# A chain of gated FFNs, attention and experts on one core: where cond's other-type half weights are loaded, which queue copies attention's values, when cond2's gate starts, and how the last tile ends

## The chip, the cores and the metric

The kernel runs on one core of a Trainium2 chip. A core has a matrix engine (TensorE, PE, with its weight loads shown as PEld), three elementwise engines (VectorE, DVE; ScalarE, ACT; GpSimd, POOL), and SyncE (SP), which here only issues DMA transfers. The letter q behind an engine's name marks its queue: instructions that wait, branch, count or issue transfers. All engines run side by side, each through its own instructions in order; a semaphore holds an instruction back until what it needs is done. The on-chip memory is addressed by 128 partitions, and the kernel lays it out by hand as one large tile (`arena`) that is cut into areas of 1 KB on each partition.

The metric is the device time of one execution in microseconds (us): the median over several runs. The profile comes from one more execution, whose own time is given beside it.

## What is computed

4096 tokens of 256 values, as 64 batches of 64. Every batch has a type from 0 to 2. All arithmetic is float32. The reference, cut to what matters here:

```python
def cond(x, t):                       # gated FFN, shared and by type
    share = (gelu(x @ sWi0) * (x @ sWi1)) @ sWo
    expert = (gelu(x @ Wi0[t]) * (x @ Wi1[t])) @ Wo[t]
    w = softmax(relu(concat([expert[:, 0], share[:, 0]]) @ g0) @ g1)
    return expert * w[:, 0] + share * w[:, 1]

def attn(x):                          # 16 heads of 16, causal, in each batch
    ...

def cond2(x, t):                      # three shared FFNs, two experts by type
    s0, s1, s2 = (relu(x @ share_wi[j]) @ share_wo[j] for j in range(3))
    out_a = relu(x @ wi[t]) @ wo[t];  out_b = relu(x @ wi[t + 1]) @ wo[t + 1]
    expert = out_a * wa + out_b * wb
    g = softmax(relu(concat([expert[:, 0], s0[:, 0], s1[:, 0], s2[:, 0]]) @ gate_w1) @ gate_w2)
    return expert * g0 + s0 * g1 + s1 * g2 + s2 * g3

def ffn(x):                           # router of three layers, top 2 of 8 experts
    scales = softmax(relu(relu(x @ rW1 + rb1) @ rW2 + rb2) @ rW3 + rb3)
    # each expert takes a limited number of tokens, adds its bias eb2, and is
    # weighted by its scale; the results are added at the token's row
    ...

x = x + attn(cond(x, itok))
x = x + ffn(cond2(x, itok))
```

## The kernel before

**Tiling.** The tokens are taken in `NSB` = 8 blocks of 512 (called s), sorted by type beforehand, so that a block has nearly one type. Each FFN layer is a product of blocks done by Strassen's method with seven products (the tiles `p1` to `p7`, with `sa`, `sb` for second halves; a letter behind them tells the stage: c for cond's shared FFN, e for cond's expert, d for cond2's, t for its expert, r for the router, m for the experts at the end). Sums of weight blocks are needed for that. They are made once on GpSimd by `sum_half` and written to DRAM (`sums_i`, `sums_o`, `sums_si`, ...; the store is L882, on GpSimd's own queue), and read back when a layer needs them. Sums of token blocks are made by `token_sums` (L193) on two engines, `eng` and `eng2`, with GpSimd taking `t3` and `t4` in most places.

**Stages, in PE's order.** cond's shared FFN (c); then `typed(0, 0)`, a few batches that are of another type than the rest of their block ("other types", plain matmuls without Strassen: tiles `peg`, `pel`, `e`); then cond's experts (e) for the eight blocks; cond2's first shared FFN (d0); the second (d1); other types of cond2 (`p2e`, `e`); the third (d2) and the experts (t); the router; the experts at the end (`pm`, `po`), whose rows are added into the output by a scatter.

**What sets the order.** The order is written out by hand. `pipeline(items)` (L402) runs the first half of item i + 1, then what is hung on item i by `hook`, then the second half of item i. Work that is not of the items, above all attention (queries, keys, values, scores, softmax, mixing) and the gates, is a list of small steps, `between`. `layer` (L300) calls `tick`, which takes one step off that list and puts it between two groups of matmuls. Empty steps `(None, False)` are spacers. The argument `ticks` ("fine", "late") says where in a layer those steps are put.

**The ring of half weights.** For cond, half weights come through a ring of `NRING1` = 5 slots of seven areas from `AT_RING1`. `queue1` (L941) lists them in order: 11 of the 12 pieces of the other types (`"f"`: k, q, and one of i0, i1, o), then the experts' pieces from the DRAM sums (`"m"`), the last `"f"` piece among them, then three of cond2's shared sums. `send1` (L948) loads the next one into the next slot: SP must wait until the piece that lay there has been used, and whatever is behind on SP's queue waits with it. In `typed(0, 0)`, `more()` calls `send1` whenever half a weight is done with.

**SP's queue.** Nearly all loads and stores go through `sync_dma` (L125) on SP's queue, one behind the other; `behind_last` keeps the written order.

**Attention's values.** For each pair of batches, `values(i)` (L1273) multiplies the values with two masks on GpSimd: `vx` (L1283) is copied across partitions into `vb` by two transfers of 64 KB on SP's queue (L1286), and the rest of `vb` is written by two multiplications (L1287). `mix` (the `ov` matmuls) reads `vb`; the softmax of the same pair runs meanwhile on VectorE (its last step is L1320). There are 32 such steps in the e and d0 stages.

**cond2's gate.** `combine2` (L1460) gives 21 steps for a block; its first, `hidden` (tile `phb`), reads first tokens that were loaded from `spillt`. For s from 1, six empty steps go ahead of it (L1622).

**The end.** `down` (L1921) finishes a tile of 128 rows of an expert: VectorE adds the bias (L1930), ACT scales by the token's weight (L1931), GpSimd issues the scatter that adds into the output (L1932). The last instruction of the kernel waits for that scatter (L1993).

Of the kernel before, what the change touches and what calls it, by code (L numbers as in the profile page):

```python
# [11 lines left out]
AF = mybir.ActivationFunctionType  # L12
# [47 lines left out]
AT_SHARE = (None, AT + 28, AT)  # L60
AT_HOPS2 = ((75, 95), (AT + 60, AT + 74), (AT_RING, AT_RING + 14))
AT_XSUM2 = (AT_XSUME, AT + 88, AT + 88)
AT_KEEP2 = ((62, 89), (AT + 92, AT + 96), (AT + 106, AT + 106))
AT_PARTS, AT_GW1, AT_X1 = AT + 92, AT + 104, 93
AT_GS = (170, AT + 112)

# [20 lines left out]
def adaln_attn_ffn(ctx: ExitStack, tc: tile.TileContext, a: dict, out: bass.AP):  # L87
# [105 lines left out]
    def token_sums(eng, eng2, b):  # L193
        b11, b12, b21, b22, t1, t2, t3, t4 = (b[n] for n in BLOCKS)
        eng.tensor_sub(t1, b12, b11)  # L195
        r = eng.tensor_sub(t2, b22, t1)  # L196
        eng2.tensor_sub(t3, b22, b12)  # L197
        return r.ins, eng2.tensor_sub(t4, b21, t2).ins  # L198

    def column_blocks(t, at, sums, eng=nc.gpsimd):  # L200
# [211 lines left out]
    def hook(it, *fs):  # L412
        it.between.extend(f for f in fs if f)
# [524 lines left out]
                q.append(("m", n - 1, "o"))  # L938
        return q

    queue1 = [("f", k, q, w) for k in range(NFIX) for q in range(2) for w in ("i0", "i1", "o")]  # L941
    last = queue1.pop()
    queue1 += in_order(0, 2 * NSB) + [("s", 1, "i"), ("s", 0, "o"), ("s", 1, "o")]
    queue1.insert(queue1.index(("m", 0, "i1")) + 1, last)
    ring1, types1, share0 = {}, {}, {}
    sent1 = [0]

    def send1():  # L948
        if sent1[0] == len(queue1):
# [26 lines left out]
    def typed(st, m):  # L976


        more = send if st else send1
        ac = []  # L980
        nn = 8 if st else 4
        hs = [0]
# [1 line left out]
        def item(b, n):  # L984
# [4 lines left out]
            def hidden(w, name):  # L989
                ph = bank(f"{name}{k}_{n}")  # L990
                for ff in range(2):
                    f = 2 * (q % 2) + ff
                    for c in range(DC):
                        mm(
                            ph[:, ff * BT : (ff + 1) * BT],
                            ring[st, k, j, q // 2, w][:, c, f * P : (f + 1) * P],
                            xes[st, k][0][:, c, :], c == 0, c == DC - 1,
                        )
                if q % 2:
                    more()  # L1000
                return ph

            def first():
# [12 lines left out]
            def second(h):  # L1016
                if not ac:
                    ac.extend(pair(f"e{st}_{m}_"))
                for ff in range(2):
                    f = 2 * (q % 2) + ff  # L1020
                    for c in range(DC):
                        mm(
                            ac[c][:, cols], ring[st, k, j, q // 2, "o"][:, f, c * P : (c + 1) * P],
                            h[:, ff * BT : (ff + 1) * BT], n == 0 and ff == 0, n == nn - 1 and ff == 1,
                        )
                if q % 2:
                    more()
                if b == 1 and n == nn - 1:
                    for c in range(DC):
                        nc.scalar.copy((tp if st else tp1)[:, c, :], ac[c])  # L1030
                    keep_typed(st, NB, NFIX * GB)
# [215 lines left out]
    def attention(s):  # L1247
# [25 lines left out]
        def values(i):  # L1273


            pv = bank(f"pv{s}_{i}")
            for c in range(DC):
                mm(pv[:, 0:D], cT[:, c, i * P : (i + 1) * P], aw["v"][:, c, :], c == 0, c == DC - 1)
            vn = area(AT_VN, D)
            nc.scalar.copy(vn, pv[:, 0:D])  # L1280
            vb = area(AT_VB + 2 * (i % 2), 2, D)
            vx = area(AT_VX + i % 2, D)
            nc.gpsimd.tensor_mul(vx, vn, K.vrest.rearrange("p a b d -> p (a b d)"))  # L1283
            for j in range(2):
                own, other = slice(64 * j, 64 * j + 64), slice(64 - 64 * j, 128 - 64 * j)
                nc.sync.dma_start(out=vb[other, j, :], in_=vx[own, :])  # L1286
                nc.gpsimd.tensor_mul(  # L1287
                    vb[own, j, :], vn[own, :], K.vmask[own].rearrange("p a b d -> p (a b d)")
                )
            return vb  # L1290
# [121 lines left out]
    def shared2(s, j):  # L1412
# [9 lines left out]
        def down(g):  # L1422
# [3 lines left out]

        return layer(
            f"d{s}_{j}", 2, ups, down, lambda: xblocks["d", s], AT_HOPS2[j], part,
            lambda: keep2(s, j, part), ahead, (AT_STE, AT_ST, AT_ST2)[j], ticks="late" if j or s > 3 else "fine",
        )  # L1430

    def store(g):
# [134 lines left out]
            between.extend(no + m2 + no * 2 + m3 + no + whole)  # L1567

    hook(items[13], lambda: [send1() for _ in range(NRING1 - 1)])
    more = []  # L1570
    for s in range(NSB):
        its = typed1(s, (lambda s=s: cut_e(s + 1)) if s + 1 < NSB else lambda: cut_x1(0, 0))
# [4 lines left out]
    starts = [10 + 2 * s for s in range(NSB)]  # L1577
    items += more
    n0 = len(items) - len(more)
    hook(more[0], send1)  # L1580
    hook(items[n0 + 2], begin_attention)
    for i in range(4):
        hook(more[3 + 5 * i], lambda v=halves2[3 - i]: sum_half(*v, AT_SUM2))
# [2 lines left out]
        share1 += shared2(s, 0)  # L1586
    items += share1
    for i in range(8):
        hook(share1[2 * i], lambda v=halves2[4 + i]: sum_half(*v, AT_RING1 + 7 * 3))
    for s in range(NSB):  # L1590
        hook(items[n0 + starts[s]], lambda s=s: begin_cond(s))
    hook(more[-2], lambda: send_share0("i", 0, AT_SUM2))
    for s in range(NSB):
        for i in range(2):
            hook(share1[2 * s + i], lambda g=NI * s + 2 * i: store(g))
# [19 lines left out]
    for s in range(NSB):  # L1615
# [3 lines left out]
            hook(its[1], lambda: [fetch2(0, j) for j in range(2)])  # L1619
            hook(its[2], router_weights, lambda: fetch2(0, 2))  # L1620
        else:
            hook(its[0], lambda s=s: between.extend([(None, False)] * 6 + combine2(s - 1)))  # L1622
        if s == NSB - 1:
            hook(its[2], lambda: sum_weights(nc.gpsimd, rw[0], 4))
            hook(its[4], router_weights1)
# [295 lines left out]
    def down(e, w, us=range(NU)):  # L1921
# [3 lines left out]
        for u in us:  # L1925
# [1 line left out]
            for f in range(FC):  # L1927
                mm(po, h[:, f, u * P : (u + 1) * P], wo[:, f, :], f == 0, f == FC - 1)
            eo = area(AT_EO + (e * NU + u) % 4, D)
            nc.vector.tensor_add(eo, po, b2[:, e, :])  # L1930
            nc.scalar.activation(eo, eo, AF.Copy, scale=xr[:, u, D + 1 : D + 2])  # L1931
            nc.gpsimd.indirect_dma_start(  # L1932
                out=out_rows, out_offset=bass.IndirectOffsetOnAxis(ap=row_i[:, u : u + 1], axis=0),
                in_=eo, in_offset=None, bounds_check=NB * S - 1, oob_is_err=False,
# [62 lines left out]
```

## Time and profile before

| | before |
|---|---|
| median of three runs | 2796.5 us (2794.85 to 2796.78) |
| the profiled execution's own time | 2799.37 us |
| its span | 2797.7 us |
| mean granted clock of TensorE | 0.997 |
| stretch 430 to 500 us: PE, DVE, POOL busy | 68.24, 51.76, 20.02 of 70 us |
| stretch 710 to 780 us: PE, DVE, POOL busy | 66.44, 58.63, 22.09 of 70 us |
| SP's longest waits in total at L1286 | 89.1 us for POOL L1283, 16 times |
| duration of the issues on SP at L1286 (64) | 502 / 572 / 4471 ns (least, median, most) |
| duration of the issues on GpSimd at L1410 (24) | 540 / 552 / 575 ns |

The profile gives, for every engine, its busy time as a share of the span; a list of the waits, each with what ended it; a timeline with the idle time ahead of each group of instructions; and the chain of waits, followed back from the last instruction. The granted clock is the share of full speed that the matrix engine was allowed in a stretch. A wait is attributed to one releaser even if several were late.

### The profile page before, as it was taken

The page shows a single profiled execution, that of the slowest core. Times are in us where ns is not written, and L with a number is a line of the kernel's source. Part 1 is how long each engine was busy: PE and PEld are TensorE (multiplying, and loading weights), DVE is VectorE, ACT ScalarE, POOL GpSimd, SP SyncE. Part 2 cuts the span into 40 slices and gives each one's busy share as a digit, 9 for nine tenths or more (in the row PEclk, how much of TensorE's full clock was granted, in tenths as well). Part 3 has the DMA queues.
Part 4 walks back from the last instruction along what each step waited for, and adds up shares of the span by engine and source line. Part 5 has one row for each costly group of instructions (what it writes and reads, how often), then busy time and mean ns, then how long its engine had stood idle before and what let it go on. Part 6 is the DMA issues. An engine that isn't in the chain of part 4 may idle for free.

```text
span 2797.7 us, 38593 instructions
## 1 busy us (share of the span) xinstructions
PE 2750.0 (98%) x13881; PEld 2269.0 (81%) x13881; DVE 1625.8 (58%) x2925; ACT 834.9 (30%) x1527; POOL 1031.3 (37%) x1057
## 2 busy tenths in 40 slices
PE   9999999999999999999999999999999999999998
PEld 7888877667676778888888888888888888887776
DVE  7777456878887774544546666667543333333443
ACT  2121114544443432211222222222222222221333
POOL 4655122322323656653332332236313232224332
PEclk9999999999999999999999999999999999999999
DMA  4454464333433223563244444444300000012330
GB/s 118 160 162 139 135 222 129 119 110 110 129 111 97 87 82 126 180 199 102 92 171 129 148 140 138 138 138 138 95 16 6 6 7 8 6 44 79 90 100 2
DMA packets 240463, 294.02 MB, mean 105 GB/s; under 512 B 142648, under 2 KB 204944, under 8 KB 240144
## 3 DMA queue, kind: packets, MB, share of 16 engines
q1 hardware_dynamic: 220752, 236.16, 27.2%
q0 software_dynamic: 19296, 54.35, 5.6%
q8 instruction: 110, 1.80, 0.3%
q10 hardware_dynamic: 224, 1.05, 0.1%
q14 instruction: 81, 0.66, 0.1%
HBM read 208.80 MB, written 84.25 MB: 105 GB/s over the span
## 4 chain that ended last, share of the span: by engine, by line
PE 85%; DVE 5%; DMA 4%; issue 3%; SPq 1%; ACT 1%; POOL 1%; POOLq 0%; DVEq 0%; ACTq 0%
PE sad L119 5%; PE p5r L119 5%; PE po L119 5%; PE p1r L119 5%; PE sbd L119 4%; PE sat L119 4%; PE p1d L119 3%; PE p5d L119 3%; PE sbt L119 3%; PE p7r L119 2%; PE p6r L119 2%; PE p4r L119 2%; PE p1e L119 2%; PE p5e L119 2%; PE p5t L119 2%
## 5 line engine op out<-in xcount | busy, mean ns | idle before, releaser
L197 POOL TENSOR_TENSOR arena<-arena 128x512 f32<-128x512 f32 (+1 forms) x175 | 236.5, 1352 | 853.1 <-DVE arena L195 666.0
L198 POOL TENSOR_TENSOR arena<-arena 128x512 f32<-128x512 f32 (+1 forms) x175 | 209.8, 1199 | 29.1 <-DVE arena L196 16.9
L119 PE MATMUL sad<-arena 128*128 128x256 f32 x768 | 177.1, 380 | 0.0
L119 PE MATMUL po<-arena 128*128 128x256 f32 (+1 forms) x704 | 169.8, 399 | 0.1
L119 PEld LDWEIGHTS sad<-arena 128*128 128x128 f32 x768 | 143.6, 190 | 19.6 <-issue 1.2
L119 PEld LDWEIGHTS po<-arena 128*128 128x128 f32 x704 | 132.7, 190 | 28.6 <-issue 11.2
L119 PE MATMUL p1r<-arena 128*128 128x256 f32 x640 | 150.2, 380 | 0.0
L119 PE MATMUL p5r<-arena 128*128 128x256 f32 x640 | 149.4, 380 | 0.5 <-DVE arena L255 0.5
L1813 POOL DMA_INDIRECT xs<-arena,slot_i x64 | 62.7, 979 | 200.5 <-ACT arena L1809 107.2
L119 PE MATMUL sbd<-arena 128*128 128x256 f32 x576 | 135.2, 382 | 0.0
L119 PEld LDWEIGHTS p5r<-arena 128*128 128x128 f32 x640 | 120.9, 190 | 17.2 <-DVE arena L255 1.1
L119 PEld LDWEIGHTS p1r<-arena 128*128 128x128 f32 x640 | 120.8, 190 | 17.3 <-issue 1.2
L195 DVE TENSOR_TENSOR arena<-arena 128x512 f32<-128x512 f32 (+2 forms) x127 | 95.1, 749 | 57.4 <-ACT arena L331 35.3
L188 POOL TENSOR_TENSOR arena<-arena 128x256 f32<-128x256 f32 (+1 forms) x53 | 49.5, 934 | 201.1 <-DMA arena<-in_L_cond_Wi 48.3
L119 PEld LDWEIGHTS sbd<-arena 128*128 128x128 f32 x576 | 108.0, 190 | 17.2 <-issue 3.0
L119 PE MATMUL sat<-arena 128*128 128x256 f32 x512 | 116.7, 381 | 0.6 <-POOL arena L197 0.6
L234 ACT COPY arena<-p1d 128x512 f32<-128x512 f32 x48 | 28.1, 586 | 295.3 <-PE p1d L119 291.5
L196 DVE TENSOR_TENSOR arena<-arena 128x512 f32<-128x512 f32 (+2 forms) x127 | 109.7, 864 | 3.2
L119 PEld LDWEIGHTS sat<-arena 128*128 128x128 f32 x512 | 96.6, 190 | 14.0 <-POOL arena L197 1.0
L1932 POOL DMA_INDIRECT out<-arena,rows_i x40 | 62.0, 1551 | 120.1 <-ACT arena L1931 64.3
L331 ACT ACTIVATE arena<-arena 128x512 f32<-128x512 f32 x144 | 90.1, 628 | 45.6 <-DVE arena L266 21.7
L119 PE MATMUL p5d<-arena 128*128 128x256 f32 x384 | 99.3, 381 | 3.3 <-DVE arena L255 3.3
(427 smaller groups left out, 6312.3 us busy)
## 6 DMA issues: line engine op xcount, KB each, us to landing
arena<-sums_i SPq DMA_DIRECT2D x32, 896.0 KB
arena<-sums_2i SPq DMA_DIRECT2D x32, 896.0 KB
arena<-sums_2o SPq DMA_DIRECT2D x32, 896.0 KB
arena<-in_L_ffn_eW SPq DMA_DIRECT2D x16, 1024.0 KB
arena<-sums_o SPq DMA_DIRECT2D x16, 896.0 KB
spill<-arena SPq DMA_DIRECT2D x24, 512.0 KB
arena<-spill POOLq DMA_DIRECT2D x24, 512.0 KB, 5.7
sums_i<-arena POOLq DMA_DIRECT2D x12, 896.0 KB, 4.0
```

What stands on the lines that cost most here:

```text
L119: nc.tensor.matmul(o, lhsT=lhsT, rhs=rhs, start=start, stop=stop, skip_group_check=shared_bank)
L188: eng.tensor_add(s1, a21, a22)
L195: eng.tensor_sub(t1, b12, b11)
L196: r = eng.tensor_sub(t2, b22, t1)
L197: eng2.tensor_sub(t3, b22, b12)
L198: return r.ins, eng2.tensor_sub(t4, b21, t2).ins
L234: nc.scalar.copy(s1, wide(x[1]))
L331: nc.scalar.activation(c_out(ij), src, AF.Relu)
L1813: nc.gpsimd.indirect_dma_start(out=to.rearrange("e n w -> (e n) w"), out_offset=bass.IndirectOffsetOnAxis(ap=slot_i[:, n, i : i + 1], axis=0),
L1932: nc.gpsimd.indirect_dma_start(out=out_rows, out_offset=bass.IndirectOffsetOnAxis(ap=row_i[:, u : u + 1], axis=0), in_=eo, in_offset=None, ...
```

## The change

It has seven parts.

1. `queue1` keeps five of the other types' twelve pieces (the first four, and the last). The other seven (`parts1`) are loaded by `send_parts`, hung on `items[14]`, into seven places of four areas from `AT` on, where cond's shared weights lay. `more(k, q, w)` in `typed(0, ...)` sends a next ring piece only if the half weight just finished lay in the ring; the single `send1` hung on `more[0]` goes. The ring has 56 pieces in place of 63, so pieces fall on other slots; two places that lie over ring slots move with them (`AT_KEEP2[0]` from 62 to 48, the area of `sum_half` from the fourth slot to the second).
2. The two copies of `vx` in `values` go out on GpSimd's queue in place of SP's. GpSimd's order in a step is then: multiply `vx`, multiply for `vb`, issue, issue, multiply for `vb`.
3. cond2's gate has seven empty steps ahead of it in place of six. With the gate's 21 steps that makes 28 for a block.
4. In `token_sums`, where one engine does all four (`eng is eng2`), `t3` comes behind `t2`: GpSimd does t1, t2, t3, t4 where it did t3, t1, t2, t4.
5. `send_share0("i", 0)`, a load of `sums_si` on SP's queue, is hung two items earlier.
6. The layer d0 puts its steps "late" from block 3 on; it did so from block 4 on. Attention's last steps fall elsewhere among the matmuls there.
7. The last tile of the last expert: ACT multiplies the bias by the token's weight ahead of time, into a spare area, and one VectorE instruction multiplies the matmul's result by the weight and adds that product, in place of an add on VectorE and a scaling on ACT.

```diff
--- before.py
+++ after.py
@@ -60,7 +60,7 @@
 AT_SHARE = (None, AT + 28, AT)
 AT_HOPS2 = ((75, 95), (AT + 60, AT + 74), (AT_RING, AT_RING + 14))
 AT_XSUM2 = (AT_XSUME, AT + 88, AT + 88)
-AT_KEEP2 = ((62, 89), (AT + 92, AT + 96), (AT + 106, AT + 106))
+AT_KEEP2 = ((48, 89), (AT + 92, AT + 96), (AT + 106, AT + 106))
 AT_PARTS, AT_GW1, AT_X1 = AT + 92, AT + 104, 93
 AT_GS = (170, AT + 112)
 
@@ -194,7 +194,8 @@
         b11, b12, b21, b22, t1, t2, t3, t4 = (b[n] for n in BLOCKS)
         eng.tensor_sub(t1, b12, b11)
         r = eng.tensor_sub(t2, b22, t1)
-        eng2.tensor_sub(t3, b22, b12)
+        with tc.issue_after(r.ins) if eng is eng2 else nullcontext():
+            eng2.tensor_sub(t3, b22, b12)
         return r.ins, eng2.tensor_sub(t4, b21, t2).ins
 
     def column_blocks(t, at, sums, eng=nc.gpsimd):
@@ -938,12 +939,18 @@
                 q.append(("m", n - 1, "o"))
         return q
 
-    queue1 = [("f", k, q, w) for k in range(NFIX) for q in range(2) for w in ("i0", "i1", "o")]
-    last = queue1.pop()
+
+    parts1 = [("f", k, q, w) for k in range(NFIX) for q in range(2) for w in ("i0", "i1", "o")]
+    queue1, parts1, last = parts1[:4], parts1[4:-1], parts1[-1]
+    in_ring = [*queue1, last]
     queue1 += in_order(0, 2 * NSB) + [("s", 1, "i"), ("s", 0, "o"), ("s", 1, "o")]
     queue1.insert(queue1.index(("m", 0, "i1")) + 1, last)
     ring1, types1, share0 = {}, {}, {}
     sent1 = [0]
+
+    def send_parts():
+        for i, (_, k, q, w) in enumerate(parts1):
+            send_half(0, k, 0, q, w, AT + 4 * i)
 
     def send1():
         if sent1[0] == len(queue1):
@@ -976,7 +983,12 @@
     def typed(st, m):
 
 
-        more = send if st else send1
+        def more(k, q, w):
+            if st:
+                send()
+            elif ("f", k, q // 2, w) in in_ring:
+                send1()
+
         ac = []
         nn = 8 if st else 4
         hs = [0]
@@ -997,7 +1009,7 @@
                             xes[st, k][0][:, c, :], c == 0, c == DC - 1,
                         )
                 if q % 2:
-                    more()
+                    more(k, q, w)
                 return ph
 
             def first():
@@ -1024,7 +1036,7 @@
                             h[:, ff * BT : (ff + 1) * BT], n == 0 and ff == 0, n == nn - 1 and ff == 1,
                         )
                 if q % 2:
-                    more()
+                    more(k, q, "o")
                 if b == 1 and n == nn - 1:
                     for c in range(DC):
                         nc.scalar.copy((tp if st else tp1)[:, c, :], ac[c])
@@ -1283,7 +1295,7 @@
             nc.gpsimd.tensor_mul(vx, vn, K.vrest.rearrange("p a b d -> p (a b d)"))
             for j in range(2):
                 own, other = slice(64 * j, 64 * j + 64), slice(64 - 64 * j, 128 - 64 * j)
-                nc.sync.dma_start(out=vb[other, j, :], in_=vx[own, :])
+                nc.gpsimd.dma_start(out=vb[other, j, :], in_=vx[own, :])
                 nc.gpsimd.tensor_mul(
                     vb[own, j, :], vn[own, :], K.vmask[own].rearrange("p a b d -> p (a b d)")
                 )
@@ -1426,7 +1438,7 @@
 
         return layer(
             f"d{s}_{j}", 2, ups, down, lambda: xblocks["d", s], AT_HOPS2[j], part,
-            lambda: keep2(s, j, part), ahead, (AT_STE, AT_ST, AT_ST2)[j], ticks="late" if j or s > 3 else "fine",
+            lambda: keep2(s, j, part), ahead, (AT_STE, AT_ST, AT_ST2)[j], ticks="late" if j or s > 2 else "fine",
         )
 
     def store(g):
@@ -1567,6 +1579,7 @@
             between.extend(no + m2 + no * 2 + m3 + no + whole)
 
     hook(items[13], lambda: [send1() for _ in range(NRING1 - 1)])
+    hook(items[14], send_parts)
     more = []
     for s in range(NSB):
         its = typed1(s, (lambda s=s: cut_e(s + 1)) if s + 1 < NSB else lambda: cut_x1(0, 0))
@@ -1577,7 +1590,6 @@
     starts = [10 + 2 * s for s in range(NSB)]
     items += more
     n0 = len(items) - len(more)
-    hook(more[0], send1)
     hook(items[n0 + 2], begin_attention)
     for i in range(4):
         hook(more[3 + 5 * i], lambda v=halves2[3 - i]: sum_half(*v, AT_SUM2))
@@ -1586,10 +1598,10 @@
         share1 += shared2(s, 0)
     items += share1
     for i in range(8):
-        hook(share1[2 * i], lambda v=halves2[4 + i]: sum_half(*v, AT_RING1 + 7 * 3))
+        hook(share1[2 * i], lambda v=halves2[4 + i]: sum_half(*v, AT_RING1 + 7))
     for s in range(NSB):
         hook(items[n0 + starts[s]], lambda s=s: begin_cond(s))
-    hook(more[-2], lambda: send_share0("i", 0, AT_SUM2))
+    hook(more[-4], lambda: send_share0("i", 0, AT_SUM2))
     for s in range(NSB):
         for i in range(2):
             hook(share1[2 * s + i], lambda g=NI * s + 2 * i: store(g))
@@ -1619,7 +1631,7 @@
             hook(its[1], lambda: [fetch2(0, j) for j in range(2)])
             hook(its[2], router_weights, lambda: fetch2(0, 2))
         else:
-            hook(its[0], lambda s=s: between.extend([(None, False)] * 6 + combine2(s - 1)))
+            hook(its[0], lambda s=s: between.extend([(None, False)] * 7 + combine2(s - 1)))
         if s == NSB - 1:
             hook(its[2], lambda: sum_weights(nc.gpsimd, rw[0], 4))
             hook(its[4], router_weights1)
@@ -1927,8 +1939,15 @@
             for f in range(FC):
                 mm(po, h[:, f, u * P : (u + 1) * P], wo[:, f, :], f == 0, f == FC - 1)
             eo = area(AT_EO + (e * NU + u) % 4, D)
-            nc.vector.tensor_add(eo, po, b2[:, e, :])
-            nc.scalar.activation(eo, eo, AF.Copy, scale=xr[:, u, D + 1 : D + 2])
+            by = xr[:, u, D + 1 : D + 2]
+            if e == E - 1 and u == NU - 1:
+
+                bw = area(AT_EO + (e * NU + u + 1) % 4, D)
+                nc.scalar.activation(bw, b2[:, e, :], AF.Copy, scale=by)
+                nc.vector.scalar_tensor_tensor(eo, po, by, bw, ALU.mult, ALU.add)
+            else:
+                nc.vector.tensor_add(eo, po, b2[:, e, :])
+                nc.scalar.activation(eo, eo, AF.Copy, scale=by)
             nc.gpsimd.indirect_dma_start(
                 out=out_rows, out_offset=bass.IndirectOffsetOnAxis(ap=row_i[:, u : u + 1], axis=0),
                 in_=eo, in_offset=None, bounds_check=NB * S - 1, oob_is_err=False,
```

## The prediction

> **What bounds the kernel now.** First the head of the page: the span, the share of each engine, and the chain that ended last.
>
> ```profile
> span 2797.7 us, 38593 instructions
> PE 2750.0 (98%) x13881; PEld 2269.0 (81%) x13881; DVE 1625.8 (58%) x2925; ACT 834.9 (30%) x1527; POOL 1031.3 (37%) x1057
> PE 85%; DVE 5%; DMA 4%; issue 3%; SPq 1%; ACT 1%; POOL 1%; POOLq 0%; DVEq 0%; ACTq 0%
> ```
>
> TensorE (PE) is the bound: 2797.7 - 2750.0 leaves 47.7 us without a matmul, start and end among them. The diff changes none of PE's work, so it can only gain from holes and from the half clock behind a long hole. So next the list of PE's waits, cut to those that the diff touches or could touch (what was waited for; us in total, times, longest):
>
> ```profile
> PE pel L119 <- DMA arena<-in_L_cond_Wi: 5.1, 1, 5.1
> ...
> PE ov L119 <- DMA arena<-arena: 2.9, 4, 1.1
> PE p6c L119 <- POOL arena L196: 2.5, 2, 2.0
> PE ov L119 <- ACT arena L1316: 2.0, 1, 2.0
> PE p1d L119 <- DMA arena<-sums_si: 1.9, 1, 1.9
> PE sae L119 <- POOL arena L197: 1.8, 1, 1.8
> PE phb L119 <- DMA arena<-spillt: 1.8, 2, 1.3
> ...
> PE phb L119 <- issue: 1.3, 1, 1.3
> ```
>
> One line or two for each edit; each is priced below from the timeline around it.
>
> **1. cond's other types out of the ring.** Seven half weights no longer wait for ring slots. The chain of waits before 356 is SP's queue: a block of eight 512 KB reads of `spill` (L126, 338.02 to 348.2), then the last half weight at 349.74, which takes 6.23 us to land. PE around it (start, us, instruction, count, idle before):
>
> ```profile
> 356.11 3.75 PE L119 MATMUL pel<-arena 128*128 128x256 f32 x8 [5.09 <-DMA arena<-in_L_cond_Wi]
> 359.65 2.70 PE L119 MATMUL e<-arena 128*128 128x256 f32 x6
> ...
> 363.92 1.89 PE L119 MATMUL pel<-arena 128*128 128x256 f32 x8
> ```
>
> The hole is 5.09 us. Behind it eight matmuls take 3.75 instead of 1.89 and six take 2.70 instead of 1.46 (the same six at 380.10): 1.86 + 1.24 = 3.1 us of low clock. Together -8.2. The new loads go to the areas of the shared weights, free after cond's last item, near 307 us; seven times 512 KB at the 272 GB/s seen in the window 350 to 364 is 13.5 us, so they have landed by about 328 us. Before, the pieces went out from 324.71 to 349.74 for use up to 356, so the cover is 20 us for the last and some microseconds for the first. What waits on SP behind them is a 0.38 us load (309.78) and stores at 323.44, both after the release. If the place came free late, the 8.2 would stay. What is late next: `pha` at 434.48 waits 1.48 for `spillt`, and stays.
>
> **2. The values' copies on GpSimd's queue.** SP loses 64 issues, GpSimd gets them, between its own multiplications (L1283, L1287). Now a copy stands behind whatever SP holds. First the SP queue, then PE, then the window with its granted clock ahead of DMA share and GB/s:
>
> ```profile
> 561.29 1.21 SPq L1286 DMA_DIRECT2D arena<-arena  x2
> ```
> ```profile
> 566.22 0.87 PE L119 MATMUL ov<-arena 128*32 128x64 f32 x16 [2.02 <-ACT arena L1316]
> ...
> 567.93 1.91 PE L119 MATMUL pv<-arena 128*128 128x256 f32 x4
> ```
> ```profile
> 566.20:570.60 4.40, 4.35 (x28) 3.23 (x30) 2.31 (x6) 1.49 (x3) 0.00 (x0) 0.61 0.98 343
> ```
>
> The wait is put down to ACT, but these copies, behind full DMA queues, landed at 566.1 and 566.4, just as `ov` starts: they end it. Waits for copies: 2.0 + 2.9 = 4.9 us. The clock of 0.61 over 4.40 us costs 4.40 x 0.39 = 1.7 (four `pv` take 1.91, four of the kind elsewhere 1.13). Together -6.6. In the later steps vx is ready 8 to 14 us before SP issues the copy (617.8 against 631.7); issued at vx, it has that much more time.
>
> The Trainium skill, "TensorE: Matmul & The Clock Gate", Part 1, has the clock halved only after an idle window of about 3.4 us. The row above disagrees, 0.61 after a hole of 2.02 us; by the rule this part would be worth 4.9 and the time 1.7 us longer.
>
> Against it stands GpSimd's time for an issue: 0.55 us by the nearest rows (L1410 552 ns, L882 573 ns), 64 x 0.55 = 35 us. In the attention stretches of 70 us GpSimd is busy 19 to 22 us, so its own 2 x 0.55 a step lie in idle time. The cost could come by VectorE, busy 57 of 70 us there:
>
> ```profile
> 719.06 5.33 DVE L1320 TENSOR_TENSOR arena<-arena,sm 128x512 f32<-128x512 f32 x2
> ```
> ```profile
> 719.38 0.58 POOL L882 DMA_DIRECT2D sums_si<-arena  x1 [0.30 <-POOL arena L191]
> ```
> ```profile
> 721.32 1.13 PE L119 MATMUL sae<-arena 128*128 128x256 f32 x4 [1.78 <-POOL arena L197]
> ```
>
> One of the two L1320 took 4.73 us (median 0.683) while GpSimd issued a store, and PE lost 1.78 and then 1.22 (`plga`, 724.53). Two other holes stand beside such issues: `p5d` at 931.58 (1.43) and 1014.95 (1.41). That is 5.8 us of PE in 38 issues of L882, and nothing in 24 of L1410. So 64 copies cost between 0 and 64 x 5.8 / 38 = 9.8. I take +3, nearer to L1410: these copies are small (64 KB) and have over 10 us in hand.
>
> **3. `send_share0` earlier, the gate later, t3 behind t2.** The load of `sums_si` goes out at 846.70 and ends PE's wait at 858.00; two items earlier is far more than 1.92 us: -1.9. The gate (`phb`, L1460 on) comes one tick later; a tick carries about four matmuls of 0.43 us, 1.7 us, more than the longest wait of 1.30: -3.1 for the three waits (1.30 at 1715.03, 1.28 at 1791.05, 0.48 at 1866.49). Its steps now fill all ticks of a stage, so a slip has nowhere to go; its fetches keep their place on SP. In `token_sums` on GpSimd the order:
>
> ```profile
> 80.70 1.17 POOL L197 TENSOR_TENSOR arena<-arena 128x256 f32<-128x256 f32 x1
> ```
> ```profile
> 84.08 1.13 PE L119 MATMUL p6c<-arena 128*128 128x256 f32 x4 [2.04 <-POOL arena L196]
> ```
>
> t3 (1.17) leaves the way to t1 and t2: -1.2 of that hole; the rest (the store's issue and t1, t2) stays.
>
> **4. Last tile in one step.** ACT's 0.51 leaves the way from the last matmul to the last scatter. But the chain at the end goes by the scatter before (start, us, what):
>
> ```profile
> 2786.86 2.72 DMA out<-arena,rows_i
> ...
> 2789.62 0.51 issue
> ```
>
> The last scatter (2790.36) follows that landing by 0.78, as the one before followed its own (2786.08 to 2786.86). Between -0.5 and +0.5 (a new ACT product, made before it is wanted); I take 0, since the spacing repeats.
>
> **5. What shifts.** Attention's remainder in the last pass is placed anew (`ticks="late"` from s = 3), one ring piece stands behind fetches, and the DVE holes (`p5c`, `p5d`, `sae`) come where chance puts them: 0, bounds -3 and +3 (that is the 721 event once more or once less).
>
> **Sum.** -8.2 - 6.6 + 3 - 1.9 - 3.1 - 1.2 = -18.0. The profiled execution took 2799.37 us, 1.67 around its span: 2799.4 - 18.0 = 2781.4. It lies 2.9 over the median of 2796.5; against that, **2778.5**. Own range: +6.8 (copies at 9.8), +-3, and 2.9 for the choice of execution: 2773 to 2788.
>
> **Rivals.**
> (a) GpSimd's issues starve VectorE in the 32 steps of the values. The 719 event is the price, 3.0 us; without the +3 the gains are 21.0, so from 7 steps on nothing is won, from 9 on (27) it is slower by over 0.2%, and at ten, -21 + 30, it is 2805. For: VectorE is 82% busy. Against: 24 issues of L1410 passed without it. The Trainium skill, "SBUF — State Buffer", section "Who interferes with whom", has an exclusive port of VectorE and GpSimd: an operation of VectorE with two SBUF inputs and one of GpSimd that reads SBUF block each other. The 4.73 us agrees, no row shows the lock itself. 0.09.
> (b) The waits for the copies pass to the next releaser (ACT's copies at L1316, DVE): the 6.6 is not had, 2785. For: that 2.02 is put down to ACT. Against: the landing times. 0.12.
> (c) Ring pieces that come later run dry. The i1 pieces of the later passes now follow eight `spillt` copies on SP, with 4.5 to 5 us left (issue 537.4, landing 542, use 547.0). Five of them late by 3 us each: 2793. For: SP's blocks of eight took 10 us at 338. Against: positive margin in every one. 0.07.
> (d) It doesn't do what it says: the parts' place is free too late, or its loads block SP, and the 8.2 stays: 2787. Against: 13.5 us of loading in 20. 0.05.
> (e) The holes at 721, 931 and 1015 go by the shift (-5.8) and the copies cost nothing (-3): 2770. 0.09.
>
> **How the numbers follow.** Forecast 0.58, rivals as given. 0.2% is 5.6 us, about what a measurement here can tell from none. Faster (under 2790.9): 0.58 + 0.12 + 0.05 + 0.09 = 0.84; same: (c), 0.07; slower: (a), 0.09. The range goes from (e) less 2 to (c): 2768 to 2793; (a) and some tails are left out.
>
> **What would show it.** No wait of `pel` near 350, and the clock full there; no `ov` wait over 0.3; `p1d` near 840 and `phb` without a hole; GpSimd's L1286 at about 0.55 us with L1320 near 0.68 beside it. The forecast is wrong if L1320 or other VectorE operations stretch beside L1286, if `e` or `p5e` wait for `sums_i`, or if `pel` still waits for `in_L_cond_Wi`.

## The result, and the profile after

The changed kernel takes 2779.15 us (median of six runs, 2776.67 to 2783.43), the kernel before 2796.64 in the same series (six runs, 2793.12 to 2799.43). The ratio is 0.9941, with a 95% interval from 0.9928 to 0.9954: between 13 and 20 us faster. The profiled execution took 2776.67 us, the fastest of the six. The profiled one of before, 2799.37, belongs to the earlier series and is as slow as the slowest of these six. So the two traces differ by more (22.7 us of span) than the medians (17.5).

The head of the page after:

```profile
span 2775.0 us, 38560 instructions
...
PE 2743.6 (99%) x13881; PEld 2265.6 (82%) x13881; DVE 1628.1 (59%) x2925; ACT 835.7 (30%) x1527; POOL 1065.5 (38%) x1121
```

PE still has 13881 matmul records, and 31.4 us of the span without one in place of 47.7. Its busy time fell too, by 6.4 us, with the same work: less of it ran at the low clock. Of PE's waits these are the ones that answer to the list of before:

```profile
PE pha L119 <- DMA arena<-spillt: 1.7, 1, 1.7
PE ov L119 <- ACT arena L1349: 1.6, 1, 1.6
PE p6r L119 <- DVE arena L196: 1.5, 6, 0.3
PE plga L119 <- DVE gha L1186: 1.4, 1, 1.4
PE sae L119 <- DMA arena<-sums_o: 1.3, 2, 1.0
```

`pel`, `p1d` and `phb` are gone; `ov` is not released by a copy any more in this list. Two kinds are new: six short ones of `p6r`, and two of `sae` for `sums_o`, a piece of the ring. Not shown are two kinds at the start, `px` (4.3, before 4.2) and one of 3.6, where PE came early to a step of the sort, and three of `ov` (1.8 in all) for which the profile names no releaser. The place of the 5.09 us hole, in PE's timeline (start, us, instruction, count):

```profile
351.23 1.89 PE L119 MATMUL peg<-arena 128*128 128x256 f32 x8
352.96 1.89 PE L119 MATMUL pel<-arena 128*128 128x256 f32 x8
354.68 1.89 PE L119 MATMUL e<-arena 128*128 128x256 f32 x8
```

Every group of eight takes 1.89 and follows the last without idle time. The last `pel` starts at 352.96, against 363.92 before; the first `peg` had started at 310.7, against 313.3. So this stage gave 8.3 us.

Where the 22.7 us between the two traces came from, by the starts of the same matmuls: 2.6 in cond's shared stage (not from the edits, see below), 8.3 in the other types, 7.4 from there to the first `p1d` (839.68 against 858.00), 1.6 up to cond2's gate, 3.1 at the gate (three `phb` holes), minus 1.6 from there to the last `po`, most of it in the router, and 1.4 behind the last matmul.

### The profile page after: what moved, and what is told of

It is laid out like the page before. It is cut to its first block, busy times and chain, and to the rows that moved or that the text cites. A ratio compares the mean times of both kernels' runs of the same rounds, so it can differ in the third digit from the quotient of the medians.

```text
span 2775.0 us, 38560 instructions
## 1 busy us (share of the span) xinstructions
PE 2743.6 (99%) x13881; PEld 2265.6 (82%) x13881; DVE 1628.1 (59%) x2925; ACT 835.7 (30%) x1527; POOL 1065.5 (38%) x1121
## 4 chain that ended last, share of the span: by engine, by line
PE 89%; DVE 4%; DMA 2%; issue 2%; SPq 1%; ACT 1%; POOL 1%; POOLq 0%; DVEq 0%; ACTq 0%
PE sad L119 6%; PE po L119 5%; PE p5r L119 5%; PE p1r L119 5%; PE sbd L119 4%; PE sat L119 4%; PE p5d L119 3%; PE sbt L119 3%; PE p1d L119 3%; PE p7r L119 2%; PE p6r L119 2%; PE p4r L119 2%; PE p5t L119 2%; PE p1t L119 2%; PE sac L119 2%; PE p5c L119 2%
## 5 line engine op out<-in xcount | busy, mean ns | idle before, releaser
L195 POOL TENSOR_TENSOR arena<-arena 128x256 f32<-128x256 f32 (+1 forms) x55 | 45.1, 820 | 245.5 <-ACT arena L1663 79.8
L119 PEld LDWEIGHTS p5r<-arena 128*128 128x128 f32 x640 | 120.8, 190 | 17.5 <-DVE arena L256 1.5
L188 POOL TENSOR_TENSOR arena<-arena 128x256 f32<-128x256 f32 (+1 forms) x53 | 48.9, 924 | 182.3 <-DMA arena<-in_L_cond_Wi 45.3
L332 ACT ACTIVATE arena<-arena 128x512 f32<-128x512 f32 x144 | 90.3, 628 | 42.3 <-DVE arena L267 22.7
```

What stands on the lines that cost most here:

```text
L119: nc.tensor.matmul(o, lhsT=lhsT, rhs=rhs, start=start, stop=stop, skip_group_check=shared_bank)
L188: eng.tensor_add(s1, a21, a22)
L332: nc.scalar.activation(c_out(ij), src, AF.Relu)
```

## The experiments

Twelve kernels ran, each in five rounds beside the kernel before. The table gives medians and ratios to that kernel in the same series. The changed kernel stood at 0.9941 in its own series; it was not timed again in the later ones.

| kernel | us | before | ratio, 95% interval |
|---|---|---|---|
| parts_alone | 2795.03 | 2795.99 | 0.9997, 0.9987 to 1.0007 |
| copies_alone | 2796.98 | 2795.99 | 1.0000, 0.9989 to 1.0010 |
| small_three | 2794.87 | 2795.99 | 0.9998, 0.9988 to 1.0008 |
| tile_and_late | 2798.19 | 2795.99 | 1.0012, 1.0002 to 1.0022 |
| both_parts_copies | 2786.14 | 2796.64 | 0.9962, 0.9949 to 0.9975 |
| copies_pinned | 2789.20 | 2796.64 | 0.9971, 0.9958 to 0.9984 |
| copies_twice | 2808.03 | 2796.64 | 1.0036, 1.0022 to 1.0050 |
| copies_on_sp | 2795.30 | 2796.64 | 0.9999, 0.9986 to 1.0011 |
| issues_more | 2796.47 | 2794.53 | 1.0008, 0.9998 to 1.0017 |
| late_back | 2783.83 | 2794.53 | 0.9958, 0.9944 to 0.9971 |
| fetch_later | 2785.76 | 2794.53 | 0.9967, 0.9955 to 0.9979 |
| t3_back | 2781.76 | 2795.21 | 0.9950, 0.9936 to 0.9964 |

**Each part alone.** The first four put one part, or a few, into the kernel before.

parts_alone has the first part of the diff and nothing else; its core:

```diff
+    queue1, parts1, last = parts1[:4], parts1[4:-1], parts1[-1]
...
+    hook(items[14], send_parts)
...
-    hook(more[0], send1)
```

> The kernel before with part 1 alone (the seven half weights in a place of their own, and the two places that move with the ring's slots). My theory: no wait of pel near 350, full clock there, about -8.2 us against the kernel before, so a ratio near 0.997. Rival: the hole only moves to the next load that SP holds up (pha near 434, or sae waiting for sums_o), and less than 4 us is left.

copies_alone:

```diff
-                nc.sync.dma_start(out=vb[other, j, :], in_=vx[own, :])
+                nc.gpsimd.dma_start(out=vb[other, j, :], in_=vx[own, :])
```

> The kernel before with part 2 alone (the values' copies on GpSimd's queue). My theory: -6.6 of waits and clock, +3 of GpSimd against VectorE, -3.6 in all (ratio 0.9987). Rival one: GpSimd's issues cost nothing, -6.6 (0.9976). Rival two: GpSimd's issues stretch VectorE's operations, 0 or slower, with L1320 over 2 us in several steps. Rival three: the waits of ov pass to ACT's copies, about 0 to -2 with ov waits of the same sum.

small_three:

```diff
-        eng2.tensor_sub(t3, b22, b12)
+        with tc.issue_after(r.ins) if eng is eng2 else nullcontext():
+            eng2.tensor_sub(t3, b22, b12)
...
-    hook(more[-2], lambda: send_share0("i", 0, AT_SUM2))
+    hook(more[-4], lambda: send_share0("i", 0, AT_SUM2))
...
-            hook(its[0], lambda s=s: between.extend([(None, False)] * 6 + combine2(s - 1)))
+            hook(its[0], lambda s=s: between.extend([(None, False)] * 7 + combine2(s - 1)))
```

> The kernel before with the gate a step later, send_share0 two items earlier and t3 behind t2. The forecast's terms: -3.1 -1.9 -1.2 = -6.2 (ratio 0.9978). From the profile after a rival: t3's order also removes three p5c holes in cond's stage (0.72, 1.72, 0.94), so -9.5 (0.9966), with no p5c wait on VectorE near 109, 154 and 194. If those holes are chance, they or others like them are there in this trace.

tile_and_late:

```diff
-(AT_STE, AT_ST, AT_ST2)[j], ticks="late" if j or s > 3 else "fine",
+(AT_STE, AT_ST, AT_ST2)[j], ticks="late" if j or s > 2 else "fine",
...
+                nc.scalar.activation(bw, b2[:, e, :], AF.Copy, scale=by)
+                nc.vector.scalar_tensor_tensor(eo, po, by, bw, ALU.mult, ALU.add)
```

> The kernel before with the last tile in one step and the layer d0 late from block 3. Forecast: 0 within 3 us (ratio 0.999 to 1.001); the last scatter still follows the landing of the one before by about 0.78 us. Rival: the placing of attention's last steps closes or opens holes of p5d near 930 and 1015, up to 3 us either way; and if ACT's 0.51 was on the way, the stretch from the last matmul to the end is shorter by it.

None of them was measurably faster, and the last was slower by 0.6 to 6 us. Added up they come to about +1 (-1.0, +1.0, -1.1, +2.2), where all together give -17.5. For the two large parts the traces show where gain is lost again. In parts_alone the hole at 350 is gone, as forecast, but a later one opens. PE's timeline of parts_alone:

```profile
487.48 1.13 PE L119 MATMUL sae<-arena 128*128 128x256 f32 x4 [2.81 <-DMA arena<-sums_o]
```

and SP's queue before it:

```profile
464.31 10.12 SPq L126 DMA_DIRECT2D arena<-spillt  x8
475.62 0.38 SPq L126 DMA_DIRECT2D arena<-sums_i  x1
476.11 1.23 SPq L1297 DMA_DIRECT2D arena<-arena  x2
477.58 0.39 SPq L126 DMA_DIRECT2D arena<-sums_i  x1
478.21 0.35 SPq L126 DMA_DIRECT2D arena<-sums_o  x1
```

The same stretch of SP's queue in the kernel before:

```profile
475.25 10.50 SPq L126 DMA_DIRECT2D arena<-spillt  x8
486.00 0.50 SPq L126 DMA_DIRECT2D arena<-sums_i  x1
486.60 1.22 SPq L1286 DMA_DIRECT2D arena<-arena  x2
488.05 0.39 SPq L126 DMA_DIRECT2D arena<-sums_o  x1
```

In parts_alone the piece that `sae` needs stands behind eight loads of `spillt`, two copies and two other pieces; it lands at 487.4. The ring's order moved by one piece, so three pieces now come behind that block where two did. With the clock behind the hole, 4.3 us of the 8.2 are given back there. The copies' wait at 561 is longer (2.77 in place of 2.02), but the clock stays full behind it, so nothing more is lost there. This does not yet give the median of -1.0: the trace is of the fastest execution of parts_alone (2790.27) and ends 9.1 us ahead of the trace of before. What takes the rest in the other executions, no trace shows.

copies_alone loses at the same place for another reason. PE's timeline of copies_alone, and the window with its granted clock ahead of DMA share and GB/s:

```profile
483.56 2.75 PE L119 MATMUL sbe<-arena 128*128 128x256 f32 x12
492.00 2.05 PE L119 MATMUL sae<-arena 128*128 128x256 f32 x4 [5.69 <-DMA arena<-sums_o]
```
```profile
492.00:497.70 5.70, 5.70 (x28) 3.89 (x28) 0.00 (x0) 0.59 (x1) 0.00 (x0) 0.50 0.00 0
```

5.69 us of hole and then half the clock: against the kernel before, 10.1 us are lost within 20 us. The weights are not late here (they land at 491.9, before at 494.4); the matmul is early. In the kernel before it stands behind `p4e`:

```profile
493.01 1.13 PE L119 MATMUL p4e<-arena 128*128 128x256 f32 x4
493.98 0.60 PE L1332 MATMUL ppT<-ident,arena 128*128 128x128 f32 x4
494.42 1.13 PE L119 MATMUL sae<-arena 128*128 128x256 f32 x4
```

The order of the engines' instructions is settled when the kernel is built, and in copies_alone this one product was put 76 matmuls further forward; PE's order is otherwise the same. Behind 500 the gains are there: 3.9 us at the hole of 566, then 0.8 near 637 and near 779, 2.3 up to the first `p1d` and 1.0 near 908, where the `ov` and `p1d` holes had been, with 1.1 lost near 725 and about 2 near 1015.

**Do the two parts need each other, and is it that one product?** both_parts_copies joins the edits of the first two. copies_pinned is copies_alone with the product held where it was:

```diff
                 for p in ("p1", "p6"):
-                    product(p)
+                    with tc.issue_after(pinned["p4e2_11"]) if (name, g) == ("e2", 1) else nullcontext():
+                        product(p)
```

copies_on_sp is the changed kernel with the copies back on SP's queue. copies_twice is a try at the price of GpSimd's issues:

```diff
-                nc.gpsimd.dma_start(out=vb[other, j, :], in_=vx[own, :])
+                for _ in range(2):
+                    nc.gpsimd.dma_start(out=vb[other, j, :], in_=vx[own, :])
```

> The kernel before with parts 1 and 2 together, nothing else. Singly they measured -1.0 and +1.0 us. Theory one (they need each other: alone, each meets a late ring piece near 490 that gives its gain back, 4.3 and 10.1 us there; together sae waits under 1.5 us there): -8.2 - 9.6 + 1 to 4, about -15, ratio 0.9935 to 0.996. Theory two (single effects add): 0 within 3 us.

> The kernel before with part 2 alone, and one product of sae (block 2, second item) held behind the p4 of its item, so that the matrix engine's order is that of the kernel before. Theory one (part 2 alone loses its gain only because that product was moved some 30 matmuls forward, ahead of its weights): the 5.69 us wait near 492 goes, and the kernel is 7 to 10 us under the one before (ratio 0.9965 to 0.9975). Theory two (the copies on GpSimd's queue cost by themselves): 0 within 3 us, with the wait at another instruction.

> The changed kernel with the copies back on SP's queue, all else as changed. Additive theory (part 2 alone was worth nothing): as the changed kernel within 3 us, 2779. Theory of the shared queue: sae near 487 waits 2.5 to 3 us again and loses some clock (4.3), ov waits near 561 and in four later places come back (6 to 9), so 2789 to 2792.

> The changed kernel with each of the 64 copies issued twice on GpSimd's queue (the second writes the same bytes again). It doubles GpSimd's issues and the small transfers. The forecast's price of GpSimd's issues against VectorE was +3 (bounds 0 and 9.8), so +3 us against the changed kernel, 2782 in all; if the issues are free, +0 to +1; if they starve VectorE, up to +10, with L1332 or other operations of VectorE over 2 us beside L1298.

Theory one holds for copies_pinned, and in direction for both_parts_copies. Together the parts give -10.5 (interval -7 to -14) where their sum singly is 0; the expected -15 was too much, and its trace has a `sae` wait of 3.1 near 562 besides the 1.0 near 483. With the product held, the copies alone give -7.4 (-4 to -12), PE's order is that of the kernel before, and this matmul starts without a wait:

```profile
490.64 0.60 PE L1334 MATMUL ppT<-ident,arena 128*128 128x128 f32 x4
491.08 1.03 PE L119 MATMUL sae<-arena 128*128 128x256 f32 x4
```

Taking the copies out of the changed kernel costs 16 us (2795.3), not 0, and more than the 10 to 13 expected: `sae` waits 2.7 near 490 and `ov` 2.8 near 564, as in parts_alone. So on SP's queue the copies and the ring's pieces hold each other up. The first part lets PE run earlier, and alone it meets a late piece; the second gets the pieces out earlier. The second does not need the first: alone it lost only by the product that moved. What the first adds to it is the difference of -10.5 and -7.4, about 3 us with intervals that overlap. No run takes part 1 alone out of the changed kernel.

copies_twice was far slower than any theory had it, 29 us over the changed kernel. GpSimd's timeline of copies_twice, and PE's waits:

```profile
560.78 0.54 POOL L1299 DMA_DIRECT2D arena<-arena  x1 [4.48 <-DMA arena<-arena]
```
```profile
PE ov L119 <- DMA arena<-arena: 11.4, 4, 3.5
```

The second transfer writes the same bytes, so GpSimd held it until the first had landed, 4.48 us here, and the other copy of the step stood behind it. That is a wait in a queue. So this run does not price the issues.

**The price of the issues, what is left near 485, and parts 6 and 4.** issues_more gives the changed kernel 64 more transfers without that wait:

```diff
                 nc.gpsimd.dma_start(out=vb[other, j, :], in_=vx[own, :])
+                nc.gpsimd.dma_start(out=aside[2 * (i % 4) + j], in_=vx[own, :])
```

late_back puts `s > 3` back:

```diff
-ticks="late" if j or s > 2 else "fine",
+ticks="late" if j or s > 3 else "fine",
```

fetch_later moves the loads of `spillt` of blocks 1 to 7 behind the three ring pieces, with the product near 490 held as above:

```diff
-            fetch_typed(0, s)
+            if s == 0:
+                fetch_typed(0, s)
...
     def begin_cond(s):
+        if s:
+            fetch_typed(0, s)
```

t3_back:

```diff
-        with tc.issue_after(r.ins) if eng is eng2 else nullcontext():
-            eng2.tensor_sub(t3, b22, b12)
+        eng2.tensor_sub(t3, b22, b12)
```

> The changed kernel with 64 more transfers of 64 KB issued on GpSimd's queue, each beside one of the copies, into a place in device memory that nobody reads (extra work, without the wait of one copy for the other that the doubled copies had). The forecast's price of the issues: +3 us (bounds 0 and 9.8) against the changed kernel's 2779, so 2782. If issues cost nothing on the path: 2779 to 2780, and VectorE's busy sum grows by less than 5 us. If they starve VectorE: over 2785, with VectorE's operations stretched beside L1298.

> The changed kernel with the layer d0 late from block 4 again (part 6 undone). From the run of the last tile with part 6 (+3.4 us against the kernel before): if that was part 6, this is about 3 us faster than the changed kernel, 2776, with p5d waiting near 1000 and no ov wait over 1.2 near 1008. If part 6 only trades one hole for another, 2779 within 2.5.

> The changed kernel with fetch_typed of blocks 1 to 7 put behind the three ring loads that it holds up on SP's queue (hung on begin_cond), and the product of sae near 490 held where it is in the changed kernel. If late ring pieces behind that block are what is left near 485 and 546: the sae wait of 0.96 and the ov wait of 1.01 go, with some clock, so 2 to 4 us faster, about 2776. If the fetch is then late for pha (20 us in hand before, some 10 then), a wait of pha appears in blocks 1 to 7 and it is slower.

> The changed kernel with t3 ahead of t1 and t2 on GpSimd again (part 2 of the order alone undone, the edit in token_sums). The forecast's term: 1.2 slower than the changed kernel, 2780. From the traces: the hole of 2.04 at 84 that the term came from is missing in six traces, five of them without the edit, and the edit brings six holes of p6r in the router (1.5 in all), which are in no trace without it; so 1 to 2 us faster, 2777 to 2778, and no p6r wait on VectorE past 2000. Either is under what five rounds tell apart; the holes in the trace decide.

issues_more came to 17 us over the changed kernel by medians of two series, and by neither theory. VectorE was not starved: its busy sum is 1632.6, 4.5 us more. PE's waits in that trace, then ACT and GpSimd around the longest:

```profile
PE p4d L119 <- ACT arena L1293: 4.7, 1, 4.7
...
PE plga L119 <- DVE gha L1187: 3.5, 1, 3.5
PE sc L119 <- ACT arena L1293: 3.3, 6, 1.0
```
```profile
925.39 0.37 ACT L1293 COPY arena<-pv 128x256 f32<-128x256 f32 x1 [5.66 <-POOL arena L1301]
```
```profile
922.39 0.59 POOL L1299 DMA_DIRECT2D arena<-arena  x1
922.97 0.57 POOL L1300 DMA_DIRECT2D aside<-arena  x1
923.54 0.52 POOL L1299 DMA_DIRECT2D arena<-arena  x1
924.05 0.53 POOL L1300 DMA_DIRECT2D aside<-arena  x1
924.64 0.72 POOL L1301 TENSOR_TENSOR arena<-arena,vmask 64x256 f32<-64x256 f32 x1
```

The second multiplication of a step stands behind all its issues, in this case four times 0.55 us. ACT's copy of the next values waits for it (`vn` must be read first), `p4d` waits for ACT, and so do six `sc`. Two issues a step, as in the changed kernel, still fit: there is no wait of PE for ACT L1292, the same copy, in its trace. In fetch_later two issues did not fit in one place: `p5d` waits 2.98 at 896 for the same copy (L1295 there), where GpSimd had also waited 1.14 for a transfer. The other 3.5, at `plga`, is not from the copies: a VectorE operation of 0.68 us stretched there to 4.83, as at 719 before. Of the 19.6 us between the spans of this trace and that of the changed kernel, some 7 lie at `p4d` and the low clock behind it, 4.5 at `plga`, 2.4 behind the last matmul (see the last section), and the rest in short waits.

late_back is 4.7 us over the changed kernel by medians of two series (10.7 against 17.5 under before), but the two intervals overlap, so part 6 stays unsettled; tile_and_late, with part 6 and the last tile in the kernel before, went the other way. In the traces part 6 trades a `p5d` hole near 1006 (1.41) for an `ov` hole near 1008 (1.61).

fetch_later was half right: both `sae` waits are gone, and no `pha` wait appears in blocks 1 to 7. But `ov` at 552 still waits 1.1, two more of `ov` near 700 (1.2 and 1.1) and the one of `p5d` at 896 are there. By the ratios it is slower than the changed kernel, not faster: 0.9967 with an interval (0.9955 to 0.9979) that does not meet that of 0.9941 (0.9928 to 0.9954). t3_back cannot be told from the changed kernel by time (0.9950 against 0.9941). Its list has no `p6r` wait past 2000. Those six waits, 1.5 us in all, are listed in all seven traces with the edit; in the seven without it there are six gaps of 0.12, too short for the list. The expectation counted wrongly there: the hole at 84 is missing in four of the earlier traces without the edit (parts_alone, copies_pinned, both_parts_copies, tile_and_late), and is there, with 1.45, in issues_more, which has it. In t3_back itself it is missing too. The list of t3_back also has a wait of `sae` for `sums_o` of 2.96 at 568: late ring pieces are not over.

No kernel of these beat the changed one.

## Why the prediction was right, and where only its sum was

Forecast 2778.5, measured 2779.15; -18.0 forecast, -17.5 measured. Step by step:

- **Part 1, -8.2: shown at its place.** From the first `peg` over 300 matmuls PE takes 65.2 us in all nine traces with the edit, 73.4 before and 72.1 to 72.6 in the four others without it. So it is 6.9 to 8.2 us; the forecast had the largest of them. But the forecast had 0 for the ring piece behind the fetch block, and looked for late pieces among i1; the late one was `sums_o` (and the load at 537.4, from which it took the margin, is itself one of `sums_o`). It costs 4.3 alone and about 0.9 at 485 in the trace of the changed kernel. Rival (c) had the right mechanism with another piece and too high a price.
- **Part 2, -6.6 for the waits and clock: shown**, -7.4 with the product held. Rival (b) falls with it: `ov` waits 0.8 in all in that trace, 5.2 before. That the part was worth 0 alone was not foreseen at all: the forecast priced only what an edit does where it stands, and not what it does to the order of another engine.
- **The +3 for GpSimd against VectorE: the term that was wrong.** In copies_pinned VectorE was busy 1623.2 us, before 1625.8: the 64 issues added nothing to it. The price came from a misread row. At 719 the store's issue was over at 719.96, and the stretched L1320 went on until 724.4, beside GpSimd's sums and multiplications:

```profile
719.99 1.28 POOL L197 TENSOR_TENSOR arena<-arena 128x512 f32<-128x512 f32 x1
721.21 1.27 POOL L198 TENSOR_TENSOR arena<-arena 128x512 f32<-128x512 f32 x1
722.43 0.72 POOL L1283 TENSOR_TENSOR arena<-arena,vrest 128x256 f32<-128x256 f32 x1
723.12 1.86 POOL L1287 TENSOR_TENSOR arena<-arena,vmask 64x256 f32<-64x256 f32 x2
```

   In parts_alone an operation of the same line (L1331 there) takes 2.83 at 713.6 with no issue beside it. Where the copies are on GpSimd's queue, the first of their issues is what such a stretch ends with. In issues_more, VectorE and then GpSimd:

```profile
706.56 4.83 DVE L1329 TENSOR_TENSOR arena<-arena,mx 128x512 f32<-128x512 f32 x1
711.32 0.68 DVE L242 TENSOR_TENSOR arena<-p6e,arena 128x512 f32<-128x512 f32 x1
```
```profile
709.44 0.72 POOL L1296 TENSOR_TENSOR arena<-arena,vrest 128x256 f32<-128x256 f32 x1
710.12 0.72 POOL L1301 TENSOR_TENSOR arena<-arena,vmask 64x256 f32<-64x256 f32 x1
710.79 0.55 POOL L1299 DMA_DIRECT2D arena<-arena  x1
```

   In the nine traces of this kind, 17 VectorE operations between 440 and 1050 were stretched by over 0.6 us into a step's copies, and all 17 ended 0.60 to 0.63 us after the first copy's issue began. So rival (a) falls: by these rows the stretch belongs to GpSimd's arithmetic, not to its issues. It still costs something in the changed kernel: L1332 takes 2.82 at 706 (`plga` waits 1.4), L1327 takes 1.74 at 542 and 1.76 at 1005, and `ov` waits 1.01 at 547 and 1.61 at 1008, behind a copy of ACT that stands in its queue behind the step that reads L1327's result. So two signs that the forecast named, no `ov` wait over 0.3 and L1320 near 0.68 beside the copies, were not met. A step has a price when the issues are doubled, but by ACT waiting behind GpSimd's queue, a chain that the forecast did not follow when it said that the issues lie in idle time.
- **`send_share0` -1.9 and the gate -3.1: the holes are gone** in the traces with these edits (839.68: `p1d` without idle time; no `phb` wait), and 3.1 to 3.5 us are gained at the gate against the trace of before. In the three traces with the copies moved but not the gate, the stretch from the first `phb` to the router is already 2.2 to 2.6 us shorter than before, and the gate's edit takes another 2.1 to 3.1. By time, small_three, which has t3's edit too, was -1.1 (-3.4 to +2.2), under the -5 of these terms: `p5d` near 924 and 1010 waited 1.9 each there (1.4 before), with low clock behind both.
- **t3, -1.2: wrong.** Of the seven traces without the edit only two have the hole at 84 (2.04 and 0.88), and the edit lengthens the `p6r` waits: from the router's first matmul to the last of all it is 799.1 to 799.7 us without it and 800.4 to 800.9 with it.
- **Last tile, 0: +0.46.** From the end of the last matmul to the last scatter's issue it is 1.85 to 1.89 us in the six traces with the edit and without extra issues, 1.37 to 1.41 in the six without it. ACT's new product waits for the spare area and stands ahead of the scaling of an earlier tile:

```profile
2761.28 0.51 ACT L1946 ACTIVATE arena<-arena 128x256 f32<-128x256 f32 x1 [3.08 <-DMA out<-arena,rows_i]
2761.70 0.49 ACT L1950 ACTIVATE arena<-arena 128x256 f32<-128x256 f32 x1
```

   This delays a scatter, and each of those that follow waits for the landing of the one before.

So the total is right in part by luck, because errors cancel: +3 not paid and 1.8 at the end not foreseen (below), against 1.2 of t3 not had, 1.5 of `p6r`, 0.9 of `sae` and 0.5 of the last tile. That makes -18.7, inside the interval of the measured -17.5. By time the runs show -10.5 for parts 1 and 2 together, and that all but 1.3 is lost when the copies go back to SP's queue. Where the other 7 us come from, no run shows by time: parts 3 to 5 alone gave -1.1, 6 and 7 alone +2.2, and the changed kernel without part 6 -10.7. Rival (d) is out, since pel's hole went; of (e) the holes at 931 and 1015 partly went, the one at 721 did not (`plga` 1.4).

## What to carry to other kernels

Price a transfer that leaves a shared queue with what stands behind it there, and look in the built order for an instruction of another engine that moves: one product put forward cost 10 us and hid a gain of the same size. When an operation is stretched, look at all that ran beside it until it ended, and not only at what began with it. Test parts together as well as singly, since two edits that each measure as nothing were worth 10 us together. A hole in one trace is a term of the forecast only if a second trace shows it.

## What the runs showed of the hardware that was not expected

The end of the program got shorter by 1.8 us. GpSimd's drain in the list of queue instructions of the last line, before and after (ns: least, median, most):

```profile
L1993 POOLq DRAIN  x3: 46/109/6742, 2790.1 to 2797.4; - x3
```
```profile
L2012 POOLq DRAIN  x3: 46/109/4952, 2769.2 to 2774.7; - x3
```

The longest takes 6.74 us in all five traces with 198 transfers issued by GpSimd, 4.95 in all seven with 262, and 6.46 in the two with 326, and the program ends behind it. Why it depends on the number so, the runs do not say.

The clock halved after shorter holes than expected: in small_three a hole of 1.86 us at 924 was followed by 3.9 us at 0.56, while one of 1.43 at 931 before was not. Over the fourteen traces, the mean granted clock in the 4 us behind a hole of PE was 1.00 for all 46 holes of 1.2 to 1.78 us, 0.57 to 0.68 for 15 of the 30 of 1.81 to 2.77 us and 1.00 for the others, and 0.50 to 0.66 for 16 of the 17 from 2.81 us on. By the Trainium skill, "TensorE: Matmul & The Clock Gate", Part 1, an idle window of about 3.4 us is needed; the trace disagrees. And the holes of cond's shared stage come and go: short VectorE operations stretch beside GpSimd's work, such as this one before, of a kind that takes 0.17 elsewhere:

```profile
150.67 2.41 DVE L681 TENSOR_SCALAR arena<-arena 128x24 f32<-128x24 f32 x1
```

Twelve of the fourteen traces have one to five `p5c` holes between 100 and 240, 1.6 to 5.0 us in sum; the changed kernel's and issues_more have none. That is part of why single executions of one kernel differ by 7 us and more.
